# Layer 2's tiles in two pools: a graph network kernel on one Trainium2 core

## The chip, the core and the metric

The kernel runs on one core of one Trainium2 chip. The core has a matrix engine (PE, with its weight loads shown apart as PEld), a vector engine (DVE), a scalar engine (ACT), a general engine (POOL, which also issues the gathers of rows by index), and SyncE (SP), which issues the plain DMAs. All engines work from their own queues in order and wait for one another by semaphores. The on-chip memory (SBUF) has 128 partitions; a tile takes the same bytes in each, so one number, the offset within a partition, says where it lies. The metric is device time in microseconds, median of several runs.

## What is computed

Four graph layers in turn on 4096 nodes with 512 features and 65,536 edges, each `x = x + layer(relu(layernorm(x)))`. The change touches layer 2, which builds a message for every edge and adds it up by destination:

```python
edge_feat = jnp.concatenate([x[src], x[dst], edge_attr], axis=-1)
h = mish(edge_feat @ W1 + b1)
messages = mish(h @ W2 + b2)
agg = jax.ops.segment_sum(messages, dst, num_segments=x.shape[0])
u = mish(jnp.concatenate([x, agg], axis=-1) @ W3 + b3)
out = u @ W4 + b4
# then x + out, layer norm with gamma and beta
```

Here `mish(x)` is `x * tanh(softplus(x))`. Layers 0, 1 and 3 are an attention layer, a degree-normalised sum with a product, and another such sum.

## The kernel before

**Stages.** Layer 0 and layer 1 go over the edges in groups. While layer 1 sums its edges (`sum_edges`, L887 to L951, pools `edge` and `beside`), class `Between` (L992) turns each finished block of 128 nodes into what layer 2 needs. It multiplies the normed rows by three parts of the weights, `product` (L1010), and stores the results as the tables `ptab`, `qtab` and `utab` (L1022) through the two-buffer tile `pq`. Its last three blocks are finished by `the_rest`, after the edges are done: first all products for `ptab`, then all for `qtab`, then all for `utab`, whose weights are `w3a_sb`. All of this is in the pool `between`.

**Layer 2's loop.** `messages` (L1160) works on 128 groups of 4 x 128 edges, on top of the small pool `l2_w` with `w1e`, `w2_sb`, `b2_bc` and `b4_beta`. Each turn of the loop deals with several groups at once, each at another step:

- Group i+2: four gathers of rows from `ptab` into `pg` (L433), four gathers from `qtab` that add into the same `pg` (L1174), and the turning of its edge attributes into `et` (PE L1285, ACT L1287).
- Group i+1: PE multiplies the attributes by `w1e` (L1295), DVE adds the product into `pg` (L1367), and ACT begins mish with a Sigmoid into `qg` (L1328).
- Group i: Arctan and Sin finish that mish (L1361, L1334), and DVE multiplies (L1337).
- Group i-1: PE turns the rows (L1302), ACT copies them to `h_t` (L1304), PE multiplies by `w2_sb` (L422), and DVE adds the bias into `z` (L1381, L1390, L1405, L1359).
- Group i-2: ACT's second mish in `t`; DVE multiplies `z` (L1397, L1403).
- Group i-3: DVE splits `z` in two halves of precision in `parts` (L1315, L1316) and builds `oh` (L428); PE adds the messages up (L1322), and DVE adds them into `acc` (L445).

Beside it, `places` (L1197) prepares the counting of edge pairs on DVE in `src_of`, `dst_of`, `same` and `of_pair`, and `shifted` (L1142, L1145, L1147) adds biases to stored rows through `rows_mid`, one block in four groups. `pg` has four buffers, `h_t` four, `et`, `qg`, `z` and `parts` two, `t`, `oh` and `rows_mid` one.

**What sets the order.** In this loop the order of PE, ACT, DVE and POOL is the written one (`manual_schedule`); SP's is the compiler's. A new tile on bytes of an earlier one waits for that tile's users: pools lie on top of one another like a stack, a pool's tiles in order of first use, and `reuse_waits="tile"` lets each tile wait only for the users of tiles on its own bytes. When layer 1 ends, its pools are released, and layer 2's lie on the same bytes, `l2_w` lowest.

**After the loop,** `layer2_ends` takes the bytes of layer 2's pools in the same way: below them lies the pool `pairs` (23,904 bytes), then `l2_end_w` with `w3_sb` (8 KB), `w4_sb` (8 KB) and `gamma_bc` (2 KB), then `u_sb`, `h2_sb`, `x2_sb` and the rest. PE turns the summed rows (L1482) and multiplies by `w3_sb` (L1496).

Of the kernel before, what the change touches and what calls it, by code (L numbers as in the profile page):

```python
# [10 lines left out]
F32 = mybir.dt.float32  # L11
BF16 = mybir.dt.bfloat16
F32R = mybir.dt.float32r
I32 = mybir.dt.int32
# [6 lines left out]
P = 128  # L21
# [13 lines left out]
def kernel(  # L35
# [24 lines left out]
    N, D = x.shape  # L60
# [3 lines left out]
    NB = N // P  # L64
    W = E // P

    U = 4
    NG = W // U
# [37 lines left out]
    d_loc = keep_pool.tile([P, W], F32, name="d_loc")  # L106
# [318 lines left out]
    def one_hots(pool, loc, t0, n, bufs=None, ids=None, dtype=F32):  # L425

        oh = pool.tile([P, n, P], dtype, name="oh", bufs=bufs)
        nc.vector.tensor_tensor(oh, (row_i if ids is None else ids).unsqueeze(1).to_broadcast([P, n, P]),  # L428
                                loc[:, t0:t0 + n].unsqueeze(2).to_broadcast([P, n, P]), op=OP.is_equal)
        return oh  # L430
# [683 lines left out]
    def fetch_attributes(g):  # L1114
        eg = eg_pool.tile([P, U, DE], F32, name="eg")
        nc.sync.dma_start(eg, edge_attr[g * U * P:(g + 1) * U * P].rearrange("(q j) d -> q j d", j=U))
        return eg
# [31 lines left out]
    with ExitStack() as l2:  # L1149
# [8 lines left out]
        shifted = Shifted(wp)  # L1158
        @with_exitstack
        def messages(ctx, begun):  # L1160
            lp = ctx.enter_context(tc.tile_pool(name="l2", bufs=2, reuse_waits="tile"))
            lps = ctx.enter_context(tc.tile_pool(name="l2_ps", bufs=2, space=PSUM, reuse_waits="tile"))

            def fetch_rows(i):
                pg = lp.tile([P, U, D], F32, name="pg", bufs=4)
                for j in range(U):
                    gather(pg[:, j, :], ptab, d_src[:, i * U + j:i * U + j + 1])
                    put_pairs(i, j % 2)
                return pg

            def add_rows(i, pg):
                for j in range(U):
                    t = i * U + j
                    nc.gpsimd.indirect_dma_start(  # L1174
                        out=pg[:, j, :], out_offset=None, in_=qtab,
                        in_offset=bass.IndirectOffsetOnAxis(ap=d_dst[:, t:t + 1], axis=0), compute_op=OP.add)
                    put_pairs(i, j == 1)

            AT = MULTIPLE
            LONG = AT + W + 1  # L1180
            src_of, dst_of, same = (lp.tile([P, LONG], F32, name=name, bufs=1) for name in ("src_of", "dst_of", "same"))
            of_pair = lp.tile([P, W], I32, name="of_pair", bufs=1)
            dump = lp.tile([P, 3], F32, name="dump", bufs=1)
            main = slice(AT, AT + W)
            place, times = same.bitcast(I32)[:, :MOST], dst_of[:, :MOST]
# [104 lines left out]
            def attribute_products(et, js):  # L1290
                made = []
                for j in js:
                    ps = lps.tile([P, D], F32, name="small_ps", bufs=4)
                    half = slice((j % 2) * DE, (j % 2 + 1) * DE)
                    nc.tensor.matmul(ps, et[half, j // 2, :], w1e[half, :], start=True, stop=True)  # L1295
                    made.append(ps)
                return made

            def turn_h(j, h):
                h_ps = lps.tile([P, KC, P], F32, name="tr_ps")  # L1300
                for k in range(KC):
                    nc.tensor.transpose(h_ps[:, k, :], h[:, j, k * P:(k + 1) * P], ident)  # L1302
                h_t = lp.tile([P, KC, P], F32, name="h_t", bufs=4)
                nc.scalar.copy(h_t, h_ps)  # L1304
                return h_t

            def second_product(h_t):
                m_ps = lps.tile([P, D], F32, name="m_ps")
                product(m_ps, h_t, w2_sb)
                return m_ps  # L1310

            def in_parts(m):

                parts = lp.tile([P, 2, 2, D], F32R, name="parts", bufs=2)
                nc.vector.tensor_copy(parts[:, 0], m)  # L1315
                nc.vector.tensor_sub(parts[:, 1], m, parts[:, 0].bitcast(F32))  # L1316
                return parts
# [15 lines left out]
            def end_mish(i):  # L1333
                nc.scalar.activation(qg, qg, AF.Sin, bias=half_pi, scale=-2.0)  # L1334
                for k in range(2):
                    half = slice(2 * k, 2 * k + 2)
                    nc.vector.tensor_mul(h[i][:, half], h[i][:, half], qg[:, half])  # L1337

            fetched, rows, h, z, h_t, et = dict(begun), {}, {}, {}, {}, {}
# [3 lines left out]
            for i in range(-2, NG + 3):  # L1343
                now = lambda k: 0 <= k < NG
                if i > 0:
                    for _ in range(4):
                        next(placing, None)
                assert i + 2 < PUT_FROM or next(placing, 1)
                if now(i + 2):
                    rows[i + 2] = fetch_rows(i + 2)  # L1350
                if now(i + 4) and i + 4 >= len(begun):
                    fetched[i + 4] = fetch_attributes(i + 4)
                if now(i + 2):
                    add_rows(i + 2, rows[i + 2])
                if now(i - 1):
                    hh = h.pop(i - 1)
                    h_t[0], h_t[1] = turn_h(0, hh), turn_h(1, hh)
                if now(i - 2):
                    nc.vector.tensor_add(z[i - 2][:, 3, :], ps3, b2_bc)  # L1359
                if now(i):  # L1360
                    nc.scalar.activation(qg, qg, AF.Arctan)  # L1361
                    if not i:
                        end_mish(i)
                if now(i + 1):
                    nxt = rows[i + 1]
                    for j, ps in enumerate(attribute_products(et.pop(i + 1), range(U))):
                        nc.vector.tensor_add(nxt[:, j], nxt[:, j], ps)  # L1367
                if now(i + 2):
                    et[i + 2] = turn_attributes(fetched.pop(i + 2))
                if now(i - 1):  # L1370
                    ps = second_product(h_t.pop(0))
                if now(i - 2):
                    mz = z[i - 2]
                    t = lp.tile([P, U, D], F32, name="t", bufs=1)
                    nc.scalar.activation(t, mz, AF.Sigmoid, scale=-1.0)
                if now(i - 3):
                    done = z.pop(i - 3)
                    parts = [in_parts(done[:, :2]), in_parts(done[:, 2:])]
                if now(i - 1):
                    zz = z[i - 1] = lp.tile([P, U, D], F32, name="z", bufs=2)  # L1380
                    nc.vector.tensor_add(zz[:, 0, :], ps, b2_bc)  # L1381
                if now(i - 3):
                    oh = one_hots(lp, d_loc, (i - 3) * U, U, bufs=1, dtype=F32R)
                if now(i - 1):
                    h_t[2], h_t[3] = turn_h(2, hh), turn_h(3, hh)
                if now(i - 2):
                    nc.scalar.activation(t, t, AF.Arctan)
                if now(i - 1):
                    ps = second_product(h_t.pop(1))
                    nc.vector.tensor_add(zz[:, 1, :], ps, b2_bc)  # L1390
                if now(i - 3):
                    ps = lps.tile([P, D], F32, name="small_ps", bufs=4)
                    add_messages(ps, range(U), oh, parts)
                    add_window(i - 3, d_bi, d_half, row_at, ps)
                if now(i - 2):
                    nc.scalar.activation(t, t, AF.Sin, bias=half_pi, scale=-2.0)
                    nc.vector.tensor_mul(mz[:, :2], mz[:, :2], t[:, :2])  # L1397
                if now(i - 1):
                    ps = second_product(h_t.pop(2))
                if now(i) and i:  # L1400
                    end_mish(i)
                if now(i - 2):
                    nc.vector.tensor_mul(mz[:, 2:], mz[:, 2:], t[:, 2:])  # L1403
                if now(i - 1):
                    nc.vector.tensor_add(zz[:, 2, :], ps, b2_bc)  # L1405
                    ps3 = second_product(h_t.pop(3))
                if now(i) and i % (NG // NB) == 0:
                    shifted.load(lp, i // (NG // NB))
                if now(i) and i % (NG // NB) == 2:
                    shifted.put(i // (NG // NB))  # L1410
                if now(i + 1):
                    qg = begin_mish(i + 1)

        messages(begun)

    ztab = dram.tile([N, D + 2], F32, name="ztab")
# [475 lines left out]
```

## Time and profile before

| | |
|---|---|
| median of 3 runs | 5047.97 us (5046.94 to 5050.79) |
| profiled execution, its time | 5048.26 us |
| profiled execution, its span | 5046.5 us |
| mean granted PE clock | 0.981 of full speed |
| busy share of the span | PE 95%, DVE 74%, ACT 71%, POOL 62% |
| last product of layer 1's edge loop (L944) | over by 1650 us |
| last product of `Between` (L1015) | over at 1684.8 us |
| first gather of layer 2 (L433 into `pg`) | 1685.1 us |
| PE busy 1650 to 1685 us, 1685 to 1716 us, 1716 to 1743 us | 29.0 of 35, 15.2 of 31, 23.0 of 27 |
| last split of `z` in layer 2's loop (L1316) | 4254.0 us |

The shares of busy time are means over stages with different limits, so they say little about a border between two stages. For that the timeline is read, which lists instructions in order of time with the idle time of the engine before each and what ended it. In these listings L12 is line 12 of the kernel, SPq and POOLq are the queues of DMAs, and the name of the engine or transfer behind `<-` is inferred from semaphores: where several were waited for, it is the one that came last by the profile.

### The profile page before, as it was taken

What the parts mean: (1) busy time and instruction counts of PE and PEld (TensorE: products, weight loads), DVE (VectorE), ACT (ScalarE), POOL (GpSimd) and SP (SyncE); (2) the same over time, 40 slices, a digit from 0 to 9 for tenths busy, and PEclk for the clock granted to TensorE, in tenths of its full rate; (3) what the DMA queues carried; (4) which work ended last, traced back from release to release, by engine and by line L of the source; (5) the groups of instructions that cost most, each with busy time, mean ns of one, the idle gap of its engine ahead of it and who ended that gap; (6) DMA issues with size and microseconds to landing.
All of it is one profiled execution on the core that took longest, in us unless ns stands there. A gap on an engine that the chain in (4) does not pass through costs nothing. (4 is left out here: it accounts for less than half of the span.)

```text
span 5046.5 us, 58005 instructions
## 1 busy us (share of the span) xinstructions
PE 4816.8 (95%) x17250; PEld 2696.7 (53%) x17250; DVE 3737.9 (74%) x6402; ACT 3584.0 (71%) x5465; POOL 3138.4 (62%) x2650
## 2 busy tenths in 40 slices
PE   6889999789999799999999999999999998999999
PEld 4477777444555345555555555555555554557444
DVE  8689999577777388987888888888878886762443
ACT  1167777577777378888888888888888886774554
POOL 0077777477777466677777777777777770002674
PEclk9899999899999899999999999999999999999999
DMA  7278888588888666565665656666666662545785
GB/s 227 89 231 249 250 245 240 173 254 273 270 275 267 161 127 130 121 128 124 130 132 121 133 121 131 131 122 133 123 129 131 123 132 85 159 139 180 229 244 173
DMA packets 402966, 862.51 MB, mean 171 GB/s; under 512 B 75217, under 2 KB 120274, under 8 KB 402642
## 3 DMA queue, kind: packets, MB, share of 16 engines
q0 software_dynamic: 228736, 612.98, 50.3%
q1 hardware_dynamic: 173906, 245.73, 14.8%
q8 instruction: 140, 2.29, 0.2%
q14 instruction: 184, 1.51, 0.1%
HBM read 733.26 MB, written 125.23 MB: 170 GB/s over the span
## 5 line engine op out<-in xcount | busy, mean ns | idle before, releaser
L422 PE MATMUL m_ps<-w_sb,h_t 128*128 128x512 f32 x4096 | 1823.2, 593 | 3.3 <-DVE z L1381 2.8
L422 PEld LDWEIGHTS m_ps<-w_sb,h_t 128*128 128x128 f32 x4096 | 758.4, 190 | 814.0 <-issue 802.3
L1174 POOL DMA_INDIRECT pg<-qtab,d_dst x512 | 955.8, 1867 | 162.7 <-issue 123.5
L433 POOL DMA_INDIRECT pg<-ptab,d_src x512 | 521.3, 1018 | 418.0 <-ACT h_t L1304 245.0
L433 POOL DMA_INDIRECT rows<-htab,s_dst x512 | 492.9, 963 | 401.3 <-issue 370.5
L433 POOL DMA_INDIRECT g<-ztab,d_src x280 | 269.6, 963 | 563.5 <-PE pair_tails L1600 383.4
L1304 ACT COPY h_t<-tr_ps 128x512 f32<-128x512 f32 x512 | 274.9, 589 | 435.3 <-PE tr_ps L1302 435.2
L724 PE MATMUL sum_ps<-rows,oh 128*128 128x261 f32 x2048 | 496.0, 389 | 25.6 <-DVE rows L718 25.6
L433 POOL DMA_INDIRECT g_split<-ytab,s_dst x384 | 392.9, 1023 | 174.5 <-issue 96.8
L1191 POOL DMA_INDIRECT pairs<-dst_of,same x304 | 373.3, 1228 | 95.7 <-issue 89.3
L724 PEld LDWEIGHTS sum_ps<-rows,oh 128*128 128x128 f32 x2048 | 377.1, 190 | 103.4 <-DVE rows L718 36.4
L1367 DVE TENSOR_TENSOR pg<-pg,small_ps 128x512 f32<-128x512 f32 x512 | 317.9, 681 | 129.0 <-PE small_ps L1295 106.6
L944 PE MATMUL sum_ps<-g,oh 128*128 128x512 f32 x816 | 396.0, 604 | 0.0
L907 ACT CAST parts<-g_split 128x512 fp32r<-128x512 f32 x384 | 232.3, 618 | 167.0 <-DMA g_split<-ytab,s_dst 128.8
L944 PE MATMUL sum_ps<-parts,oh 128*128 128x512 f32 x768 | 307.9, 508 | 42.0 <-ACT oh L899 36.3
L908 DVE TENSOR_TENSOR parts<-g_split,parts 128x512 fp32r<-128x512 f32 x384 | 250.4, 688 | 106.9 <-ACT parts L907 105.9
L1322 PE MATMUL small_ps<-parts,oh 128*128 128x512 f32 x1024 | 307.4, 443 | 20.0 <-DVE oh L428 20.0
L1316 DVE TENSOR_TENSOR parts<-z,parts 128x1024 fp32r<-128x1024 f32 x256 | 313.7, 1225 | 8.8
L445 DVE SCALAR_TENSOR_TENSOR acc<-small_ps,d_half,acc 128x512 f32 x256 | 192.3, 751 | 166.9 <-PE small_ps L1322 157.0
L1302 PEld LDWEIGHTS tr_ps<-ident,pg 128*128 128x128 f32 x2048 | 240.2, 141 | 141.0 <-issue 140.7
L1337 DVE TENSOR_TENSOR pg<-pg,qg 128x1024 f32<-128x1024 f32 x256 | 301.4, 1219 | 7.9 <-ACT qg L1334 7.9
L1295 PE MATMUL small_ps<-w1e,et 64*128 64x512 f32 x1024 | 266.2, 626 | 9.9 <-DMA w1e<-in_L_gnn_W_dram 6.5
(355 smaller groups left out, 9030.8 us busy)
## 6 DMA issues: line engine op xcount, KB each, us to landing
eg<-in_edge_attr_dram SPq DMA_DIRECT2D x128, 128.0 KB, 2.7
pairs<-none SPq DMA_DIRECT2D x32, 448.0 KB, 6.0
many<-pairs SPq DMA_DIRECT2D x32, 448.0 KB, 3.4
xt<-in_x_dram SPq DMA_DIRECT2D x8, 1024.0 KB, 5.8
htab<-acc SPq DMA_DIRECT2D x32, 256.0 KB, 2.0
x_row<-in_x_dram SPq DMA_DIRECT2D x32, 256.0 KB, 4.2
rows<-htab,s_dst POOLq DMA_INDIRECT x512, 3.9
x<-x_row SPq DMA_DIRECT2D x32, 256.0 KB, 3.6
```

The source lines that it names most:

```text
L422: nc.tensor.matmul(ps, h_t[:, k, :], w_sb[:, k0 + k, :], start=start and k == 0, stop=stop and k == KC - 1)
L433: nc.gpsimd.indirect_dma_start(out=dst_ap, out_offset=None, in_=table, in_offset=bass.IndirectOffsetOnAxis(ap=idx, axis=0))
L724: nc.tensor.matmul(ps[:, c, :HW], oh[:, j + k, :], rows[:, j + k, c * HW:(c + 1) * HW], start=j + k == 0, stop=j + k == GT - 1)
L944: nc.tensor.matmul(ps[:, :D], by[:, j, :], row, start=i % per == 0 and j == k == 0, stop=i % per == per - 1 and j == U - 1 and k == len(ro ...
L1174: nc.gpsimd.indirect_dma_start(out=pg[:, j, :], out_offset=None, in_=qtab, in_offset=bass.IndirectOffsetOnAxis(ap=d_dst[:, t:t + 1], axis= ...
L1191: nc.gpsimd.indirect_dma_start(out=pairs.rearrange("n d -> (n d)").unsqueeze(1), out_offset=bass.IndirectOffsetOnAxis(ap=place[:, w:w + 1] ...
L1295: nc.tensor.matmul(ps, et[half, j // 2, :], w1e[half, :], start=True, stop=True)
L1304: nc.scalar.copy(h_t, h_ps)
L1316: nc.vector.tensor_sub(parts[:, 1], m, parts[:, 0].bitcast(F32))
L1322: nc.tensor.matmul(ps, oh[:, j, :], parts[j // 2][:, k, j % 2, :], start=j == 0 and k == 0, stop=j == U - 1 and k == 1)
L1337: nc.vector.tensor_mul(h[i][:, half], h[i][:, half], qg[:, half])
L1367: nc.vector.tensor_add(nxt[:, j], nxt[:, j], ps)
```

## The change

The tiles of layer 2's loop are taken from two pools instead of one. The new pool `l2_later` is opened first, so it lies directly above `l2_w`. It takes `src_of`, `dst_of`, `same`, `of_pair`, `parts`, `t`, `z`, `oh` and `rows_mid`. The old pool `l2` keeps `dump`, `pg`, `et`, `qg` and `h_t`, and now lies above the new one. Sizes, numbers of buffers and instructions stay.

```diff
         def messages(ctx, begun):
+            later = ctx.enter_context(tc.tile_pool(name="l2_later", bufs=2, reuse_waits="tile"))
             lp = ctx.enter_context(tc.tile_pool(name="l2", bufs=2, reuse_waits="tile"))
...
-            src_of, dst_of, same = (lp.tile([P, LONG], F32, name=name, bufs=1) for name in ("src_of", "dst_of", "same"))
-            of_pair = lp.tile([P, W], I32, name="of_pair", bufs=1)
+            src_of, dst_of, same = (later.tile([P, LONG], F32, name=name, bufs=1) for name in ("src_of", "dst_of", "same"))
+            of_pair = later.tile([P, W], I32, name="of_pair", bufs=1)
             dump = lp.tile([P, 3], F32, name="dump", bufs=1)
...
-                parts = lp.tile([P, 2, 2, D], F32R, name="parts", bufs=2)
+                parts = later.tile([P, 2, 2, D], F32R, name="parts", bufs=2)
...
-                    t = lp.tile([P, U, D], F32, name="t", bufs=1)
+                    t = later.tile([P, U, D], F32, name="t", bufs=1)
...
-                    zz = z[i - 1] = lp.tile([P, U, D], F32, name="z", bufs=2)
+                    zz = z[i - 1] = later.tile([P, U, D], F32, name="z", bufs=2)
...
-                    oh = one_hots(lp, d_loc, (i - 3) * U, U, bufs=1, dtype=F32R)
+                    oh = one_hots(later, d_loc, (i - 3) * U, U, bufs=1, dtype=F32R)
...
-                    shifted.load(lp, i // (NG // NB))
+                    shifted.load(later, i // (NG // NB))
```

## The prediction

> **What bounds the kernel now.** I read the 40 slices first: PE is at 9 tenths nearly throughout, with a dip to 7 in the fourteenth slice (1640 to 1766 us), where layer 1 ends and layer 2 begins. In a stretch of steady layer 2 (2000 to 2178 us, by stage) PE is busy 176.3 of 178 us, DVE 158.1, ACT 145.4, POOL 111.1: PE sets the group's period, 19.6 us from one Sin to the next. So the change cannot shorten a group. It can shorten the start, where by the same view PE is busy 15.2 of the 31 us from 1685 to 1716, and it can harm the end, where layer 2's closing part takes the same bytes. So I read the timeline at both places. Columns: start, duration, engine, line, operation, out<-in, count, [idle before it <- who ended it].
>
> ```profile
> 1668.28 0.32 SPq L1022 DMA_DIRECT2D ptab<-pq  x1
> ...
> 1674.33 10.46 PE L1015 MATMUL pq_ps<-w3a_sb,ht_mid 128*128 128x512 f32 x24
> ...
> 1685.07 0.94 POOL L433 DMA_INDIRECT pg<-ptab,d_src  x1 [46.52 <-PE tr_ps L1285]
> ...
> 1686.65 1.20 SPq L1155 DMA_DIRECT2D w1e<-in_L_gnn_W_dram  x2
> ...
> 1691.50 5.63 PE L1295 MATMUL small_ps<-w1e,et 64*128 64x512 f32 x8 [6.49 <-DMA w1e<-in_L_gnn_W_dram]
> ...
> 1697.79 0.37 ACT L1287 COPY et<-tr_ps 128x256 f32<-128x256 f32 x1 [9.38 <-PE tr_ps L1285]
> 1697.89 12.54 SPq L1116 DMA_DIRECT2D eg<-in_edge_attr_dram  x2
> 1698.18 1.28 ACT L1328 ACT_TABLE_LOAD   x1
> 1698.96 0.69 DVE L1367 TENSOR_TENSOR pg<-pg,small_ps 128x512 f32<-128x512 f32 x1 [13.44 <-DMA pg<-qtab,d_dst]
> ...
> 1707.35 1.91 ACT L1328 ACTIVATE qg<-pg 128x2048 f32<-128x2048 f32 x1 [7.89 <-DVE pg L1367]
> ```
>
> POOL, which fetches layer 2's rows, is idle for 46.5 us. The page names PE's transposes, but the first gather does not read them. It reads `ptab`, whose last store is issued at 1668.28 and lands 2.0 us later by the list of DMA issues of this stretch, and it writes `pg`. By the sizes in the code, counted from the first byte above the persistent tiles, `pg` of group 0 lies at 24,896 to 33,088 and `w3a_sb` at 32,352 to 40,544: they share 736 bytes. `w3a_sb`'s last product ends at 1684.79, and the gather starts 0.28 us later. That is the wait that the change removes.
>
> ```profile
> 1733.91 8.80 PE L422 MATMUL m_ps<-w_sb,h_t 128*128 128x512 f32 x16 [2.83 <-DVE z L1381]
> ```
>
> One group on, PE is held 2.83 us more: the add into `z` stands on DVE behind the adds of group 2 (L1367), which wait for their gathers until 1733.16. The 16 products then take 8.80 us, where the same 16 at 4196.07 take 7.03; the weight loads are 0.85 us apart to 1737.8 and 0.43 after it.
>
> **The new places.** The lower pool holds, in order of first use, `src_of`, `dst_of`, `same`, `of_pair`, `rows_mid`, `z`, `t`, `parts`, `oh`, from 16,384 to 71,968. Layer 1's `Between` ends at 59,200, so all of `pg`, `et`, `qg`, `h_t` lies over the edge loop's buffers, whose last product (L944) is over by 1650. No instruction or DMA is added or removed; only waits change.
>
> **The gain at the start, step by step.** Call G and A the four gathers (L433) and four adding gathers (L1174) of a group.
> 1. G of group 0 starts when `ptab` has landed, about 1670.5 instead of 1685.07. With 0.95 us and a gap of 0.30 each, it ends at 1675.5. A needs `qtab`, last issued at 1675.3 and landing at 1677.3; at 1.57 plus 0.30 each it is over by 1685. POOL is then one stage ahead: it begins G of group 1 where it now begins group 0.
> 2. Late next is `w1e`. SP issues it at 1686.65, behind the last `utab` store, and the change leaves that order alone. PE's first L1295 still starts near 1691.5 and the four products end near 1697. DVE's four adds then run as the products come, to about 1697.9, not 1707.3. ACT has the copy of the next `et` (1697.79) and a table load in front, so the first Sigmoid starts at 1698.18 + 1.28 = 1699.46, not 1707.35: **7.9 us**. Arctan, Sin and the products that turn `h` follow by that much.
> 3. Group 1's adds lose their wait: the fourth, at 1719.73, waits 1.03 us for its gather. **1.0 us**.
> 4. Group 2's adds: their rows land when group 1's do now, the fourth by 1719.7; add and `z` add are then done by 1721.1. PE comes to the product that needs that bank at 1731.08 - 8.9 = 1722.2. So the gap of **2.8 us** closes, with 1 us to spare.
> 5. With no gap, the 16 products take 7.03 and not 8.80: **1.8 us**. [...]
>
> Sum 7.9 + 1.0 + 2.8 + 1.8 = 13.5 us. From group 3 on, PE is full, nothing waits for a gather (the adds at 1744.67 wait for PE only), and the lead is carried unchanged.
>
> What no row shows: `w1e`'s landing with other traffic beside it. Now it takes 4.7 us beside group 0's gathers; then it will do so beside group 1's. `eg`, of 128 KB like each half of `w1e`, takes 2.7 us by the page, so 2 us more gain is the good end; 1 us of extra crowding is the bad one. I take the row, since as many gathers stand beside it.
>
> [...]
>
> **The cost at the end.** The tiles that are used late in a group are also the last to be free, and the closing part loads its weights on top of them.
>
> ```profile
> 4205.10 0.38 SPq L412 DMA_DIRECT2D w_sb<-in_L_gnn_W_dram  x1
> ...
> 4226.67 0.37 SPq L412 DMA_DIRECT2D w_sb<-in_L_gnn_W_dram  x1
> ...
> 4254.01 1.22 DVE L1316 TENSOR_TENSOR parts<-z,parts 128x1024 fp32r<-128x1024 f32 x1
> ...
> 4265.35 7.88 PE L1496 MATMUL u_ps<-w_sb,a_t 128*128 128x512 f32 x16
> ```
>
> Now `w3_sb` (4205.10) and `w4_sb` (4226.67) lie over `pg` and start early. After it, `w3_sb` (23,904 to 32,096) lies over `rows_mid` and the `z` of even groups, read last for group 126 at 4243.2; `w4_sb`, the first `u_sb` and `gamma_bc` lie over the `z` of odd groups, read last at 4255.23. Queued behind on SP: nothing else until 4263.58. `w3_sb` then lands at 4243.3 + 5.2 (median of the two weight loads here) = 4248.5, needed at 4265.35; `u_sb`, 4 us and more after 4255.3, is needed at 4269.83; `w4_sb` by about 4262, needed at 4282.56. (All in the old clock.) Cost 0, cover 16.9 us for the first. If `w3_sb` too went only at 4255.3 and behind those 1.75 MB (4.5 us at the 390 GB/s that the DMA row shows there), with the 9.8 us to landing that layer 2's own 1 MB load took, it would land at 4269.6, and PE would wait up to 4.4 us.
>
> **Result:** 5048.0 - 13.5 = 5034.5 us. The profiled execution took 5048.26 (span 5046.5), 0.3 above the median of 5047.97, so the sum is taken off the median as it is.
>
> **Rivals.**
> - *Half of it:* rows land later than I think beside layer 2's weights (DMA share 0.93 from 1685 to 1716, half that work now still in flight), so steps 4 and 5 fail: 8.9 us, 5039. For: 1 us of slack. Against: POOL is a whole stage ahead.
> - *The end gives back* 4.4 us: 5039. Against: SP's queue is empty there.
> - *It does not do it:* the first gather truly waits for PE's transposes, as the page says: 5048. Against: et's copy (19.78 us idle until the `utab` store has read `pq`) shows the same kind of wait by bytes.
> - *Slower:* the moved tiles are slower in their new bytes in every group. One place: the products L1322 out of `parts`, 443 ns each. The like product of layer 1 (L944, also from `parts`) takes 508. Eight times 65 ns in 127 groups cost 66 us: 5100. From 13 ns a product it eats the gain. Against: DVE's add of 128x512 takes 688, 692 and 680 ns in three places of memory.
>
> **How the numbers follow.** Measurements of this kernel cannot tell less than about 0.2%, 10.1 us, from no change: faster means under 5037.9. Mine 0.60 (5032.5 with the early `w1e`, 5037.3 without step 5 and with 1 us of crowding); half of it 0.15; the end 0.08; no effect 0.09; slower 0.08. A quarter of the second and third falls under the bound: faster 0.66, same 0.26, slower 0.08. The range is 5031 to 5040.5: my case and the two beside it, with a microsecond of scatter.
>
> **What would show it.** Right: POOL's first gather near 1670.5, first Sigmoid near 1699.5, second near 1711.5, no gap before the 16 products near 1722 and 7.0 us for them, `w3_sb` issued near 4230, PE's first L1496 near 4252. Wrong: a first gather still at 1685, a late `w1e`, a group period other than 19.6, or PE idle before L1496.

## The result and the profile after

The new kernel took 5036.29 us (median of 9 runs, 5033.84 to 5041.82); the kernel before took 5048.39 us on the same chip (9 runs). The ratio is 0.9975 with a 95% interval of 0.9966 to 0.9984, so the gain is 8 to 17 us, 12.1 by the medians. The profiled execution's span fell from 5046.5 to 5034.4 us.

First the timeline of the new kernel at the border between layers 1 and 2, with the columns of the prediction. The inserted line shifts later line numbers by one.

```profile
1667.08 0.32 SPq L1022 DMA_DIRECT2D ptab<-pq  x1
...
1670.11 0.95 POOL L433 DMA_INDIRECT pg<-ptab,d_src  x1 [32.14 <-issue]
...
1673.13 10.46 PE L1015 MATMUL pq_ps<-w3a_sb,ht_mid 128*128 128x512 f32 x24
...
1677.81 1.59 POOL L1175 DMA_INDIRECT pg<-qtab,d_dst  x1 [3.00 <-DMA qtab<-pq]
...
1683.43 1.55 POOL L1175 DMA_INDIRECT pg<-qtab,d_dst  x1 [0.30 <-issue]
...
1685.28 1.00 POOL L433 DMA_INDIRECT pg<-ptab,d_src  x1 [0.30 <-issue]
1685.50 1.41 SPq L1155 DMA_DIRECT2D w1e<-in_L_gnn_W_dram  x2
...
1691.24 2.04 PE L1296 MATMUL small_ps<-w1e,et 64*128 64x512 f32 x2 [7.43 <-DMA w1e<-in_L_gnn_W_dram]
...
1693.32 0.69 DVE L1368 TENSOR_TENSOR pg<-pg,small_ps 128x512 f32<-128x512 f32 x1 [9.00 <-PE small_ps L1296]
...
1694.16 3.78 PE L1296 MATMUL small_ps<-w1e,et 64*128 64x512 f32 x6 [0.88 <-DMA w1e<-in_L_gnn_W_dram]
...
1698.59 0.37 ACT L1288 COPY et<-tr_ps 128x256 f32<-128x256 f32 x1 [14.37 <-PE tr_ps L1286]
...
1700.28 1.91 ACT L1329 ACTIVATE qg<-pg 128x2048 f32<-128x2048 f32 x1
```

POOL's first gather starts 3.0 us after `ptab`'s last store is issued and no longer waits for `w3a_sb`'s products. When those end, at 1683.59, POOL is at the last adding gather of group 0. What ends PE's idle time now is `w1e` alone, and it comes in two halves, the second 2.9 us behind the first. DVE's adds, which waited for gathers before, wait for PE.

One group on (same view):

```profile
1715.27 3.60 PE L422 MATMUL m_ps<-w_sb,h_t 128*128 128x512 f32 x8
...
1719.58 10.53 PE L422 MATMUL m_ps<-w_sb,h_t 128*128 128x512 f32 x24
...
1721.56 0.69 DVE L1368 TENSOR_TENSOR pg<-pg,small_ps 128x512 f32<-128x512 f32 x1 [1.43 <-DMA pg<-qtab,d_dst]
...
1722.17 0.68 DVE L1382 TENSOR_TENSOR z<-m_ps,b_bc 128x512 f32<-128x512 f32 x1
...
1729.94 1.04 PE L1303 MATMUL tr_ps<-ident,pg 128*128 128x128 f32 x8
```

The same place in the kernel before, around the block shown in the prediction:

```profile
1727.48 3.60 PE L422 MATMUL m_ps<-w_sb,h_t 128*128 128x512 f32 x8
...
1742.55 1.04 PE L1302 MATMUL tr_ps<-ident,pg 128*128 128x128 f32 x8
```

In this profile the gap of 2.83 us is gone: 24 products run as one block at 0.44 us each. In a second profile of the new kernel ("the change again" in the experiments) it is not quite gone:

```profile
1721.08 3.60 PE L422 MATMUL m_ps<-w_sb,h_t 128*128 128x512 f32 x8
...
1725.17 0.69 DVE L1368 TENSOR_TENSOR pg<-pg,small_ps 128x512 f32<-128x512 f32 x1 [1.54 <-DMA pg<-qtab,d_dst]
...
1726.60 7.11 PE L422 MATMUL m_ps<-w_sb,h_t 128*128 128x512 f32 x16 [1.92 <-DVE z L1382]
```

There group 2's fourth add still waits for its rows, and PE stands 1.92 us behind it. The gap comes back in part, but the 16 products take 7.11 us, 0.44 us each as in the block above.

The view by stage gives, for each stretch, its length, the busy time and number of instructions of PE, PEld, DVE, ACT and POOL, the granted clock, the DMA share and GB/s. Before:

```profile
1716.00:1743.00 27.00, 22.97 (x63) 11.49 (x64) 13.02 (x25) 12.57 (x12) 21.88 (x18) 0.85 0.80 165
```

After, in the first profile, PE is never idle from 1716 to 1743 and its granted clock is 1.00; the steady stretch is as it was, 176.35 us busy against 176.30.

```profile
1685.00:1716.00 31.00, 17.22 (x40) 7.93 (x41) 7.47 (x14) 14.04 (x12) 18.81 (x16) 0.61 0.91 254
1716.00:1743.00 27.00, 27.00 (x87) 12.99 (x86) 14.29 (x22) 19.50 (x18) 21.90 (x18) 1.00 0.85 175
2000.00:2178.00 178.00, 176.35 (x594) 90.49 (x593) 156.83 (x206) 145.28 (x117) 114.44 (x78) 1.00 0.59 124
```

The end of the loop, same timeline:

```profile
4230.23 0.38 SPq L412 DMA_DIRECT2D w_sb<-in_L_gnn_W_dram  x1
...
4242.57 0.46 SPq L412 DMA_DIRECT2D w_sb<-in_L_gnn_W_dram  x1
...
4248.28 1.94 PE L1483 MATMUL tr_a<-ident,acc 128*128 128x128 f32 x8 [1.75 <-DVE acc L445]
...
4253.08 7.88 PE L1497 MATMUL u_ps<-w_sb,a_t 128*128 128x512 f32 x16
```

`w3_sb` is issued at 4230.23, 38 us later against the last Sin than before, and the products that read it still start behind PE's transposes, not behind a DMA.

**The sum of the spans.** Layer 1's last product ended 1.20 us earlier in the new profile (1683.59 against 1684.79), which the change does not touch; five further profiles of the experiments' kernels, which leave layer 1 alone too, on chips of the same pace put it anywhere from 1683.2 to 1689.5. From there to the last Sin of layer 2 the new kernel took 2517.83 us, the one before 2529.70: **11.87 us** less. From the last Sin to the end it took 832.98 against 832.01. 1.20 + 11.87 - 0.97 = 12.10. What the change did is the 11.87, give or take the scatter of about 2 us given below.

### The profile page after: what moved, and what is told of

Its sections match the earlier page's. It is cut to its first block, busy times and chain, and to the rows that moved or that the text cites. A ratio compares the mean times of both kernels' runs of the same rounds, so it can differ in the third digit from the quotient of the medians.

```text
span 5034.4 us, 57994 instructions
## 1 busy us (share of the span) xinstructions
PE 4808.1 (96%) x17250; PEld 2695.9 (54%) x17250; DVE 3735.6 (74%) x6402; ACT 3582.7 (71%) x5465; POOL 3135.5 (62%) x2650
## 5 line engine op out<-in xcount | busy, mean ns | idle before, releaser
L1303 PE MATMUL tr_ps<-ident,pg 128*128 128x128 f32 x2048 | 266.3, 273 | 6.2 <-DVE pg L1338 6.2
```

## The experiments

All places are counted from the end of layer 1's last product (L1015) in the same profile, so that what went before drops out. That matters: the first four experiments and the last ran on chips where the stages ahead of this stretch and behind it took longer for every kernel (before: 5436.03 us, and 5503.46 in the one run beside the last). The new kernel itself was not run on those chips. The column "last Sin" is the start of Sin for group 127; two profiles of the new kernel itself differ by 1.8 us in it, so less than about 2 us is no finding.

| kernel | first gather | first adding gather | first product by `w1e` | first Sigmoid | last Sin | ratio to before (95%) |
|---|---|---|---|---|---|---|
| before | 0.28 | 5.28 | 6.71 | 22.56 | 2529.70 | 1 |
| the change | -13.48 | -5.78 | 7.65 | 16.69 | 2517.83 | 0.9975 (0.9966 to 0.9984) |
| the change again | -13.48 | -5.43 | 9.23 | 15.86 | 2519.64 | 0.9969 (0.9956 to 0.9981) |
| `pg` over `w1_sb` | -10.03 | -5.02 | 8.45 | 14.87 | 2517.43 | 0.9978 (0.9967 to 0.9989) |
| `pg` back | 0.27 | 5.27 | 6.70 | 22.96 | 2528.77 | 0.9994 (0.9982 to 1.0006) |
| `z` above | -13.48 | -5.81 | 8.61 | 15.51 | 2516.58 | 0.9959 (0.9946 to 0.9972) |
| `w1e` early | -13.67 | -4.54 | 0.84 | 11.42 | 2516.25 | 0.9957 (0.9941 to 0.9973) |
| SP's loads late | -13.48 | -5.66 | 8.15 | 15.69 | 2517.63 | 0.9973 (0.9964 to 0.9982) |
| both of these | -13.68 | -4.19 | 0.83 | 11.73 | 2521.41 | 0.9979 (0.9970 to 0.9988) |
| `parts` lowest | -13.48 | -5.27 | 7.73 | 14.32 | 2518.58 | 0.9977 (0.9969 to 0.9984) |
| group 1 behind `w1e` | -13.48 | -4.73 | 9.39 | 16.50 | 2524.28 | 0.9985 (0.9976 to 0.9994) |
| adding gathers of 0 behind `w1e` | -13.49 | 6.16 | 4.60 | 21.89 | 2530.69 | one run |

### Do the shared bytes hold the gather?

Two kernels move `pg` in other ways. The first is the kernel before with the tiles for counting pairs lifted into a pool above the rest, so that `pg`, and every tile behind it, moves down by 8.4 KB: `pg` off `w3a_sb` and onto the tile below it, `w1_sb`.

```diff
 lp = ctx.enter_context(tc.tile_pool(name="l2", bufs=2, reuse_waits="tile"))
+above = ctx.enter_context(tc.tile_pool(name="l2_above", bufs=2, reuse_waits="tile"))
...
-src_of, dst_of, same = (lp.tile([P, LONG], F32, name=name, bufs=1) for name in ("src_of", "dst_of", "same"))
-of_pair = lp.tile([P, W], I32, name="of_pair", bufs=1)
-dump = lp.tile([P, 3], F32, name="dump", bufs=1)
+src_of, dst_of, same = (above.tile([P, LONG], F32, name=name, bufs=1) for name in ("src_of", "dst_of", "same"))
+of_pair = above.tile([P, W], I32, name="of_pair", bufs=1)
+dump = above.tile([P, 3], F32, name="dump", bufs=1)
```

> Before, with one thing changed: the small pair tiles (src_of, dst_of, same, of_pair, dump) go to a pool above, so pg moves down by 8.4 KB and its first buffer lies over w1_sb alone (last read at about 1674.4) and no longer on the first 736 bytes of w3a_sb. Everything used late stays above, as before. If those 736 bytes were the whole of the wait: first gather near 1674.7, first Sigmoid near 1700, 10 to 12 us faster than before (about 5037). If the gather waits for PE's transposes, or if it is the parting into late and early tiles that brings the gain: no change, 5048.

The second is the new kernel with `pg` alone put back into the lower pool; the late tiles behind it move up by its size.

```diff
-pg = lp.tile([P, U, D], F32, name="pg", bufs=4)
+pg = later.tile([P, U, D], F32, name="pg", bufs=4)
```

> After, with pg alone put back into the lower pool behind of_pair, so that it shares some 700 bytes with w3a_sb again; et, qg and h_t stay above. If pg's bytes are the cause: first gather at about 1685 again, 5048. et's wait for the utab store is gone here and should be worth nothing, since w1e comes later. If the other tiles' places bring part of the gain: between 5037 and 5045.

Timeline of the first:

```profile
1979.40 12.59 PE L1015 MATMUL pq_ps<-w_sb,ht_mid 128*128 128x512 f32 x28
...
1991.83 10.46 PE L1015 MATMUL pq_ps<-w3a_sb,ht_mid 128*128 128x512 f32 x24
1992.26 0.95 POOL L433 DMA_INDIRECT pg<-ptab,d_src  x1 [45.93 <-PE pq_ps L1015]
```

The last product that reads `w1_sb` (shown as `w_sb`) ends at 1979.40 + 12.59 = 1991.99 us and the gather starts 0.27 us later, just as in the kernel before it started 0.28 us after the last product that reads `w3a_sb`. Timeline of the second:

```profile
1999.99 10.46 PE L1015 MATMUL pq_ps<-w3a_sb,ht_mid 128*128 128x512 f32 x24
2010.29 0.38 PE L1286 MATMUL tr_ps<-ident,eg 128*128 128x128 f32 x2
2010.72 0.94 POOL L433 DMA_INDIRECT pg<-ptab,d_src  x1 [55.08 <-PE tr_ps L1286]
```

With `pg` back, the wait and nearly all of the time are back: last Sin 0.93 us from the kernel before, within scatter, ratio 0.9994. The page again names PE's transposes as the releaser, though they are only the PE instructions that happened to end last. So the wait follows the bytes, and the place of `pg` is the whole of the gain: what else moved brings and costs nothing that these runs can tell. The first kernel lifts a few small tiles and gains as much as the change (last Sin 2517.43), although its first gather starts 3.45 us later than the change's.

### Does the late `w3_sb` cost anything at the end?

One kernel puts `z` above and `qg` below, which frees `w3_sb`'s bytes early; another puts `parts` and `oh` lowest of all, which frees them last.

```diff
-s = lp.tile([P, U, D], F32, name="qg", bufs=2)
+s = later.tile([P, U, D], F32, name="qg", bufs=2)
...
-zz = z[i - 1] = later.tile([P, U, D], F32, name="z", bufs=2)
+zz = z[i - 1] = lp.tile([P, U, D], F32, name="z", bufs=2)
```

> After, with z in the upper pool and qg in the lower one (the same 16 KB), so that w3_sb and w4_sb of the closing part no longer lie on the tile that is read last in the loop. If the late start of these loads is hidden: no change from after, 5036, though w3_sb is issued some 12 us or more earlier. If the late loads are what gives back 0.8 us at the end: 0.8 us faster, 5035.5. If they crowd the closing part more than the trace shows: 2 to 4 us faster.

```diff
+latest = ctx.enter_context(tc.tile_pool(name="l2_latest", bufs=2, reuse_waits="tile"))
 later = ctx.enter_context(tc.tile_pool(name="l2_later", bufs=2, reuse_waits="tile"))
...
-parts = later.tile([P, 2, 2, D], F32R, name="parts", bufs=2)
+parts = latest.tile([P, 2, 2, D], F32R, name="parts", bufs=2)
...
-oh = one_hots(later, d_loc, (i - 3) * U, U, bufs=1, dtype=F32R)
+oh = one_hots(latest, d_loc, (i - 3) * U, U, bufs=1, dtype=F32R)
```

> After, with parts and oh lowest of all, so that w3_sb lies on the tile that PE reads last in the loop. w3_sb can then be issued only some 45 us behind the last Sin (28.8 in after), and PE needs it at 51.7. With 5.2 us to landing it comes 0 to 1 us before it is needed, with 7 us one or two behind. Mine: 0 to 3 us slower than after. If a load of weights is never what holds the closing part up: no change.

These are places from the last Sin:

| | before | the change | the change again | `z` above | `parts` lowest |
|---|---|---|---|---|---|
| `w3_sb` issued | -9.39 | 28.81 | 28.82 | -9.47 | 44.91 |
| first product that reads it | 50.86 | 51.66 | 50.91 | 50.80 | 51.43 |
| first eight `tr_a` transposes take | 1.06 | 1.94 | 1.06 | 1.06 | 1.94 |

The products start 0.8 us later in the change's profile than before, and this looks like the price of the late load. It is not: in the second profile of the same kernel, with the load as late, they start at 50.91. The start goes with how fast PE runs the eight transposes ahead of it. Timeline of the new kernel's second profile, to be set against the 1.94 shown above:

```profile
4252.83 1.06 PE L1483 MATMUL tr_a<-ident,acc 128*128 128x128 f32 x8 [1.76 <-DVE acc L445]
```

In the first profile the granted clock was 0.50 over the 1.94 us; in the kernel before, where the eight took 1.06 us, it was 1.00 over them. So the load's place costs nothing that these profiles can tell, down to 44.91 us, 6.5 us ahead of its use.

### Can the start gain more if `w1e` comes sooner?

`w1e` is loaded ahead of layer 1's last blocks, into a tile that stands empty then (the trace has the load issued 903 us ahead of the end of L1015):

```diff
-    s_new = src_pool.tile([P, W], F32, name="s_new")
+    s_new = keep_pool.tile([P, W], F32, name="s_new")
...
+        w1e = s_new
+        for j in range(2):
+            nc.sync.dma_start(w1e[j * DE:(j + 1) * DE, :], w1[2 * D:])
         between.the_rest(3)
...
-        w1e = wp.tile([P, D], F32, name="w1e")
-        for j in range(2):
-            nc.sync.dma_start(w1e[j * DE:(j + 1) * DE, :], w1[2 * D:])
```

> After, with w1e loaded while layer 1 ends (into a persistent tile that layer 0 has done with), so that it is there when PE has turned the first attributes. My account: PE's first L1296 comes at 1684 and not 1691, the first Sigmoid at about 1689 and not 1700, but then group 1's rows (landing near 1705) and above all group 2's (1721.6) are next, and the third product of group 0 waits for them: no gain on after, 5036, give or take 2 (PE cools in the longer gap). If w1e is the only thing in the way: 6 to 10 us faster than after, 5027 to 5030.

Timeline of this kernel (its last L1015 product ends at 2012.06):

```profile
2012.90 1.99 PE L1296 MATMUL small_ps<-s_new,et 64*128 64x512 f32 x8 [0.61 <-ACT et L1288]
2013.15 1.55 POOL L1175 DMA_INDIRECT pg<-qtab,d_dst  x1 [0.30 <-issue]
...
2022.75 0.69 DVE L1368 TENSOR_TENSOR pg<-pg,small_ps 128x512 f32<-128x512 f32 x1 [3.90 <-DMA pg<-qtab,d_dst]
2023.48 1.91 ACT L1329 ACTIVATE qg<-pg 128x2048 f32<-128x2048 f32 x1 [6.51 <-DVE pg L1368]
...
2036.64 0.69 DVE L1368 TENSOR_TENSOR pg<-pg,small_ps 128x512 f32<-128x512 f32 x1 [0.93 <-DMA pg<-qtab,d_dst]
```

PE has `w1e` 6.8 us sooner than in the change, and the Sigmoid comes 5.3 us sooner. What is late next are rows: group 0's fourth adding gather is through on POOL at 2014.70, and its add starts only at 2022.75, so about 8 us pass until the rows are there. One group on, the fourth add waits for its rows as well. PE's first eight products by `w2_sb` take 5.37 us instead of 3.60, with the first weight loads 0.85 us apart and the last 0.43; the 16 of the next group take 7.11 us behind a gap of 0.99. At the last Sin 1.6 us are left of the 5.3, no more than two profiles of one kernel differ by.

Two more kernels issue the loads that nobody needs yet (`b4_beta`, the first `rows_mid`, the long rows of `src_of` and `dst_of`) from ACT's queue, the first two at i = 1 of the loop, without and with the early `w1e`:

```diff
-                nc.sync.dma_start(self.by[:, k, :], ap.partition_broadcast(P))
+        def fill(self, queue=nc.sync):
+            for k, ap in enumerate((b4, beta)):
+                queue.dma_start(self.by[:, k, :], ap.partition_broadcast(P))
...
-                if now(i) and i % (NG // NB) == 0:
+                if i == 1:
+                    shifted.fill(nc.scalar)
+                    shifted.load(later, 0, nc.scalar)
+                if now(i) and i and i % (NG // NB) == 0:
...
-                    nc.sync.dma_start(of[:, main], stab[k])
+                    nc.scalar.dma_start(of[:, main], stab[k])
```

> After, with the loads that nobody needs yet (b4 and beta, the first rows_mid, the long rows of src_of and dst_of: 1.5 MB in six DMAs) issued from ACT in turn 1 of the loop and no longer from SP right behind w2_sb. If crowding by these loads holds up the rows: the gathers of groups 1 and 2 land sooner (POOL's waits of 3.2 and 4.7 us in front of the adding gathers shrink), but the first Sigmoid stays, as w1e comes before these loads in the queue; group 2's adds no longer wait. Since PE has no gap there any more, 0 to 2 us faster than after. If the weights w2_sb alone crowd: no change. ACT's six issues could cost 1 to 2 us.

> After, with w1e early and the loads late. If w1e, then the rows under crowding are the two next limits: first Sigmoid at about 10 us behind layer 1's last product and the later ones 5 to 8 us earlier than after, 4 to 8 us faster than after. If another thing is next (the rows of group 2 at POOL's own pace: two stages of 15 us from 1.7 us on end at 31): 2 us at most, as with w1e early alone (1.6).

Alone, this leaves `w1e`'s first product at 8.15 and the last Sin where it was: these loads are not what delays `w1e`. The rows profit, since group 2's adding gathers start at 23.66 instead of 26.58, but in the change's first profile PE was not waiting for them. With both edits the first Sigmoid is early (11.73), yet the fourth add of group 2 waits 3.29 us for its rows, PE stands 4.82 us ahead of the 16 products, and these take 10.01 us. The last Sin is at 2521.41, 3.6 us behind the change and 1.8 behind its second profile; neither forecast had a loss. The new kernel was run once more beside these two and the one with `parts` lowest:

> The changed kernel itself once more, as the measure for the next three on the same chip: 12 us faster than before, with first Sigmoid about 16.7 us and the last Sin 2518 us behind the end of layer 1's last product.

Its ratio is 0.9969, and the intervals of all four overlap. No version run here is ahead of the change by more than the scatter.

### What delays `w1e`?

`w1e` came later than before in every profile with the load in its old place and group 0's adding gathers ahead of it, and later than the prediction had it. Its load is issued at about 1.9 us in every one of these kernels but the two with `w1e` early. Beside it lie the plain loads right behind it, group 1's gathers, and group 0's adding gathers right ahead of it. One kernel holds POOL at group 1's gathers until `w1e` is there:

```diff
+                if i == -1:
+                    nc.gpsimd.tensor_copy(dump[:, 2:3], w1e[:, 0:1])
                 if now(i + 2):
                     rows[i + 2] = fetch_rows(i + 2)
```

> The new kernel with one GpSimd copy of one column of w1e into the spare tile ahead of group 1's source rows, so that GpSimd holds group 1's gathers until w1e has landed; everything computed is the same. All places are counted from the end of layer 1's last product. Theory, that w1e came late because the gathers of group 1 lay beside it in the DMA queues: its first product comes back to about 6.7 us, where it was in the kernel before (7.65 and 9.23 in two profiles of the new kernel), the first Sigmoid to about 14 to 15 (16.69 and 15.86), and group 1's rows come 4 to 5 us later, so that the third Sigmoid moves to 43 to 45 (41.45 and 40.33) and the time is the same or up to 3 us more than the new kernel's: 5036 to 5039. Rival, that w2_sb's transfer, the loads of SP beside it or group 0's adding gathers delay w1e: the first product stays at 7.7 to 9.2 and only group 1 is later.

The other holds POOL one step sooner, between group 0's gathers and its adding gathers:

```diff
+                if i == -2:
+                    nc.gpsimd.tensor_copy(dump[:, 2:3], w1e[:, 0:1])
                 if now(i + 2):
                     add_rows(i + 2, rows[i + 2])
```

> The new kernel with one GpSimd copy of one column of w1e into the spare tile between group 0's gathers and its adding gathers, so that no indirect transfer is issued from about 9 us ahead of the end of layer 1's last product until w1e has landed; everything computed is the same. Holding back group 1's rows (the run before this) left w1e's first product at 9.39 us after that end. Theory, that w1e is late behind group 0's adding gathers, which the new kernel issues just ahead of it: the first product is at 6.7 us or sooner, as in the two profiles where group 0's rows came later (6.71 and 6.70), while the first Sigmoid is not earlier than about 17, since the adding gathers then start only at 6.7 and end 8 us later. Rival, that the indirect transfers have no part in it and it is the plain loads issued by SP right before and behind it: the first product stays between 7.6 and 9.4 us.

Timeline of the kernel that holds group 1 (L1015 ends at 1689.46):

```profile
1690.36 1.55 POOL L1175 DMA_INDIRECT pg<-qtab,d_dst  x1 [0.30 <-issue]
...
1691.37 1.21 SPq L1155 DMA_DIRECT2D w1e<-in_L_gnn_W_dram  x2
...
1698.85 4.81 PE L1296 MATMUL small_ps<-w1e,et 64*128 64x512 f32 x8 [9.18 <-DMA w1e<-in_L_gnn_W_dram]
...
1699.98 0.18 POOL L1351 COPY dump<-w1e 128x1 f32<-128x1 f32 x1 [8.08 <-DMA w1e<-in_L_gnn_W_dram]
1700.65 1.00 POOL L433 DMA_INDIRECT pg<-ptab,d_src  x1 [0.49 <-issue]
```

Timeline of the kernel that holds group 0's adding gathers (L1015 ends at 2076.68):

```profile
2078.54 1.20 SPq L1155 DMA_DIRECT2D w1e<-in_L_gnn_W_dram  x2
...
2081.28 4.23 PE L1296 MATMUL small_ps<-w1e,et 64*128 64x512 f32 x8 [4.37 <-DMA w1e<-in_L_gnn_W_dram]
...
2082.00 0.18 POOL L1355 COPY dump<-w1e 128x1 f32<-128x1 f32 x1 [14.10 <-DMA w1e<-in_L_gnn_W_dram]
2082.84 1.60 POOL L1175 DMA_INDIRECT pg<-qtab,d_dst  x1 [0.65 <-issue]
```

From `w1e`'s issue to PE's first product it is 2.74 us with no indirect transfer beside it, and 7.48 us with group 0's adding gathers alone. In the change's two profiles, with these and group 1's gathers, it is 5.7 and 7.4, and the four other kernels with this order lie between. In the kernel before and in the one with `pg` back, with group 0's plain gathers, it is 4.85 in both. So it is group 0's adding gathers, which were moved ahead of `w1e`, and not group 1's. The kernel with nothing beside the load was profiled once, on another chip, and the two profiles of the change differ by 1.6 us. The direction is outside that scatter; the exact price, and how these gathers hold the load up, is not known.

Holding the adding gathers back is no cure: with them behind `w1e` the first Sigmoid is at 21.89 and the last Sin at 2530.69, beside 2529.70 for the kernel before.

In the kernel that holds group 1 my theory of `w1e` fell and its rival held, and I had the cost too low as well. The third Sigmoid is at 45.65, and the last Sin is 6.45 us behind the change's and 4.64 behind its second profile's, not up to 3 (5044.83 us against 5051.05 before, ratio 0.9985). So a delay of 9.5 us to group 1's gathers gives back about half of the gain, though the first Sigmoid is as early as in the change. The waits that the prediction's step 3 removed are there again (0.58 and 1.09 us at group 1's adds). From 33.5 to 60.5 us after layer 1's end (1723 to 1750) PE is busy 26.17 of 27 us at a mean granted clock of 0.91, where the change has 27.00 of 27 at 1.00 from 32.4 to 59.4 (1716 to 1743), and a gap of 0.83 us stands ahead of the 16. POOL's lead, not the first Sigmoid alone, carries the gain.

## The prediction, point by point

The forecast was 5034.5 us with a range of 5031 to 5040.5; the median is 5036.29. The likeliest case came true: the cause and the place are right. But the sum was too large by 1.6 us against the first profile and by 3.4 against the second, and the terms do not add up as freely as I wrote them.

- **Step 1, POOL starts when `ptab` has landed.** Right in cause and place. Predicted about 1670.5, found 1670.11; the adding gathers from 1677.81 to 1684.98 where 1677.3 to 1685 stood. The times agree so well only because layer 1 ended 1.20 us sooner: from its end, the first gather was foreseen at -14.3 and came at -13.48, the first adding gather at -7.5 and came at -5.78. They started 3.0 and 3.7 us after the last store of their tables was issued, not 2.2 and 2.0. The kernels that move `pg` show that the shared bytes hold it, so the rival that the change does not do it falls.
- **Step 2, the first Sigmoid 7.9 us sooner.** This term was mis-sized: in the first profile it measured **5.9** (22.56 to 16.69). The chain is as written: four products, four adds, the copy of the next `et`, the table load, the Sigmoid. Its first link was late: the second half of `w1e` reached PE at 10.57 and not 8.56 as before, 2.0 us. I had taken the old landing time "since as many gathers stand beside it", with 1 us of crowding as the bad end. The kind or the order of the gathers decided (no run parts the two), not their number: with four adding gathers just ahead of the load it was 7.48 us from its issue to its first product, with four plain gathers beside it 4.85. The estimate used a row of the old order for a load whose neighbours the same change replaces. The 2.0 us are the worst of several, though: with the first Sigmoid at 15.86 in the second profile, and at 14.32 with `parts` lowest, the term is 6.7 and 8.2.
- **Step 3, 1.0 us at group 1's adds.** Right: from the first to the second Sigmoid the change takes 11.98 us, the kernel before 13.10, 1.1 less.
- **Steps 4 and 5, 2.8 and 1.8 us.** Right together in the first profile: PE turns `h` of group 1 at 1729.94 instead of 1742.55. That is 12.61 us sooner, of which 1.2 were there at layer 1's end and 5.9 + 1.1 are steps 2 and 3; **4.4** are left of the 4.6 foreseen. Read directly, from 1727.48 to 1742.55 before and from 1719.58 to 1729.94 after, they are 4.7. The 5037.3 in the forecast has step 5 at nothing. No run shows such a step: the 16 products took 8.80 us behind the gap of 2.83, with the granted clock at 0.50 from 1734.4 to 1737.7, and 7.11 us behind the 1.92 of the second profile.
- **The slack of step 4.** This is the reading that was most off. Group 2's fourth add was foreseen 34.9 us after layer 1's end (1719.7) and came at 37.97, and at 38.95 in the second profile. In the first profile the add into `z` ends at 1722.17 + 0.68 = 1722.85, and the 17th product is due at 1719.58 + 8 x 0.439 = 1723.09: 0.24 us of slack, not 1. In the second, PE comes 1.1 us sooner and finds the rows later, so 1.92 of the 2.83 us stay, and step 4 gives 0.9. With `pg` over `w1_sb` and with `parts` lowest, where PE is sooner still, 1.67 and 1.46 us stay. So the rival *half of it* had the right weak spot, and in the first profile the late `w1e` hid it: by these profiles, a first Sigmoid 2 us sooner would have met the rows of group 2 next.
- **POOL's gathers.** Between 1670 and 1685 they took 0.94 to 0.95 and 1.55 to 1.59 us, where step 1 had 0.95 and 1.57.
- **The end, cost 0.** Right: `w3_sb` issued at 4230.23, predicted near 4230; PE's first L1497 at 4253.08, predicted near 4252. In the rival of this part the last difference is 4269.6 - 4265.35 = 4.25 us and not 4.4; nothing hangs on it.
- **Slower through the new bytes.** Refuted: the products out of `parts` take 442 ns over the whole run where they took 443, and in the steady stretch PE is busy for the same time.

The sum 7.9 + 1.0 + 2.8 + 1.8 = 13.5 became 5.9 + 1.1 + 4.4 = 11.4 in the first profile. As the 4.4 is what was left over, this is the lead at one place; the last Sin, read apart from it, gives 11.87. In the second profile 6.7 + 1.1 + 0.9 + 1.7 (8.80 to 7.11) = 10.4 stands beside 10.06 at the last Sin. The 1.2 us of layer 1 and the 1.0 at the end belong to no step and nearly cancel. That steps 4 and 5 held in full in the first profile was luck more than foresight, as the slack shows.

## What to carry to other kernels

When an engine is idle for long at a border between two stages, compute which bytes its first instruction writes and who used them last; the releaser named by the profile may only be the engine that ended at the same time. Then move the one tile that is late: here 736 shared bytes of `pg` cost 10 to 12 us, and moving `pg` off them was enough. Ask what becomes late next: here it was `w1e`, and right behind it the rows of group 2, so a gain at the first does not add to the sum in full. When transfers move ahead of others, don't take the landing time of the ones behind them from a row of the old order, and look at the kind and the order of the transfers that now stand ahead.

## What the runs showed of the hardware

- A load of two times 128 KB reached its first reader 2.74 us after its issue with no indirect transfer beside it, and 7.48 us after four adding gathers of 128 rows each. Those gathers took 1.55 to 1.59 us each on POOL. Where the fourth add of group 0 waited for their rows, it started about 8 us after the last of them (five profiles); for groups 1 and 2 it was 4.0 to 6.4 us.
- Behind a gap of 1.46 to 1.92 us the weight loads of the 16 products were 0.43 us apart, and the products took 7.11 us (four profiles). Behind a gap of 2.83, 4.82 or 5.03 us the first loads were 0.85 us apart and the later ones 0.43, and the products took 8.8 to 10.0 us (one profile each); at the 2.83 the granted clock was 0.50 from 1734.4 to 1737.7.
- PE's speed at the same place differed between two profiles of one kernel: eight transposes took 1.94 us, at a granted clock of 0.50, or 1.06. Why, no run shows. It moved the start of a stage by 0.8 us, which could be taken for an effect of the change.
- The chips of these runs differed more than the kernels did. On the chip of the first four experiments the kernel before took 5436.03 us, 388 more than at first, but from L1015 to the last Sin these kernels took the same time as on the others (`pg` back, 2528.77, beside 2529.70 for the kernel before); the difference lies ahead of L1015's end (2010.45 us against 1684.79) and behind the last Sin (883 against 832).
